# A decoder layer with a mixture of experts: the start and the end of the expert stage rearranged

## The chip, the cores and the metric

The kernel runs on one core of a Trainium2 chip. The metric is device time in microseconds (us), the median of several executions. The kernel's engines are named as in its profile: PE is the matmul engine (PEld its weight loads), DVE is VectorE, ACT is ScalarE, POOL is GpSimd, SP is SyncE, which here only issues transfers. All data is fp32.

## The reference

The input `x` has 2 x 1024 tokens of 256 numbers. Three blocks are added to it one after the other: self-attention of its normalised rows, cross-attention to 77 context rows, and a feed-forward block with experts. Only the last one is touched by the change:

```python
probs = jax.nn.softmax(flat @ gate_W, axis=-1)           # 8 experts
topk_w, topk_idx = jax.lax.top_k(probs, TOP_K)           # the best two
topk_w = topk_w / topk_w.sum(axis=-1, keepdims=True)
combine = (one_hot(topk_idx, n_exp) * topk_w[..., None]).sum(axis=1)
out = 0.5 * gelu(flat @ shared_W + shared_b)
for e in range(n_exp):
    h = gelu(flat @ W1[e] + b1[e])                       # 256 -> 1024
    out = out + combine[:, e:e+1] * (h @ W2[e] + b2[e])  # 1024 -> 256
out = (out - mean) * rsqrt(var + 1e-5) * gamma + beta
x = x + out
```

`flat` is the layer-normalised input of the block. Every token is needed by two experts only, with two weights.

## The kernel before

**Stages.** Self-attention runs from 0 to about 540 us, cross-attention with the layer norm, the gate and the routing to 665.8, the experts to 952.7, the end to 1002.9. In the first two stages the order of each engine's instructions is written out by hand (a list of words, worked off inside `manual_schedule`); this ends at L1351, and after it a scheduler orders the instructions by their dependences and by the order of the program.

**Routing.** Tokens stand in 16 groups (`NT`) of 128. The routing gives each (token, choice) pair, 4096 in all, a slot in a list that is sorted by expert and padded to multiples of 128. For each slot `rows()` (L1275) works out with four DVE instructions `to_row`, the pair's row in the DRAM buffer `pairs`, and from it `from_row`, the token's row in the DRAM buffer `xnd` of normalised tokens. An empty slot gets a `to_row` past the end, which the write leaves out. `owner_i` has the expert of each tile, and DVE wrote it earlier.

**Tiles.** The slots are worked off in 23 tiles: 12 pair tiles of 256 slots, then 11 single tiles of 128. How many of the last three are needed depends on the data (`count_i`), so tiles 20 to 22 lie inside branches. A tile consists of

- `fetch_weights` (L1336): SP loads the tile's expert number into a register and issues three transfers, `w1` (1 MB, L1339), `w2` (1 MB, L1342) and `b2` (128 KB, L1345). There are three sets of buffers. The sets of tiles 0 and 1 are asked for ahead of the routing's last steps, the set of tile i + 2 in tile i.
- `fetch` (L1391): POOL issues one indirect transfer for every 128 slots, which gathers rows of `xnd` by `from_row` (L1396). Three buffers `xg`, two tiles ahead.
- `first_layer` (L1406): PE transposes `xg` into `px` (L1412), DVE copies it to `xgT` (L1416), 16 matmuls give `ph` (L1422), ACT takes the Gelu with the bias (L1429).
- `second_layer` (L1434), one tile behind: 8 or 16 matmuls into `po` (L1441), DVE adds the bias into `y` (L1448), POOL issues an indirect transfer that scatters `y` to `pairs` by `to_row` (L1452).

Beside the tiles stand asides: the shared expert's Gelu in tiles 1 to 4, adding `beta` to the tokens `xs` in tiles 5 to 8, and in tile 9 `weigh` (L1362), which works out the two weights `wts` of each token.

**The end.** Eight transfers of 512 KB (L1508) load the pair rows: four chunks `c` of four groups of tokens, each for the first and for the second choice, on the queues of SP and ACT. Per chunk DVE adds the weighted rows to the shared expert's output `acc` with eight `scalar_tensor_tensor` (L1516) and takes mean and variance (L144, L145); `norm_scale` follows on DVE (L136) and POOL (L137). For chunks 0 to 2 DVE works out an offset (L1526), ACT normalises (L1530), and POOL multiplies by `gamma` (L1534) and adds the tokens (L1537). Chunk 3 does all this on DVE (`affine_residual`, L208 and L212). Each chunk's output leaves as one transfer of 512 KB (L1538).

Of the kernel before, what the change touches and what calls it, by code (L numbers as in the profile page):

```python
# [8 lines left out]
F32 = mybir.dt.float32  # L9
# [5 lines left out]
P = 128  # L15
# [25 lines left out]
def decoder_kernel(  # L41
# [48 lines left out]
    xnd = dram.tile([N, D], F32, name="xnd")  # L90
    pairs = dram.tile([2 * N, D], F32, name="pairs")
# [130 lines left out]
    scrap = const.tile([P, 6048], F32, name="scrap")  # L222
# [950 lines left out]
    pair_no = number("pair_no", [[N, 2], [P, NT]], 1, 1, [P, 2, NT])  # L1173
# [19 lines left out]
    pair = rt.tile([P, NS], F32, name="pair")  # L1193
# [81 lines left out]
    def rows():  # L1275

        ppk = held["ppk"]
        nc.vector.tensor_scalar(pair, ppk, 0.0, float(2 * N + 1), ALU.is_equal, ALU.mult)
        nc.vector.scalar_tensor_tensor(pair, pair, -1.0, ppk, ALU.add, ALU.add)
        nc.vector.tensor_copy(to_row, pair)  # L1280
        nc.vector.tensor_scalar(from_row, to_row, N - 1, None, ALU.bitwise_and)
# [46 lines left out]

    with tc.tile_pool(name="ff1", bufs=1) as ff1, ExitStack() as later:
        b2s = [ff1.tile([P, D], F32, name=f"b2_{k}") for k in range(3)]
        gamma_f = load_bcast(f_gamma, "gamma_f")
        beta_f = load_bcast(f_beta, "beta_f")
        def fetch_weights(i):  # L1336
            e = nc.sync.value_load(owner_i[0:1, i : i + 1], min_val=0, max_val=E - 1)
            w1, w2, b2 = w1s[i % 3], w2s[i % 3], b2s[i % 3]
            nc.sync.dma_start(  # L1339
                out=w1, in_=f_w1[bass.ds(e, 1)].rearrange("o (kc p) f -> p (o kc) f", p=P)  # L1340
            )
            nc.sync.dma_start(  # L1342
                out=w2, in_=f_w2[bass.ds(e, 1)].rearrange("o (hc p) f -> p (o hc) f", p=P)
            )
            nc.sync.dma_start(out=b2, in_=f_b2[bass.ds(e, 1)].to_broadcast([P, D]))  # L1345
            return w1, (w2, b2)

        weights = {i: fetch_weights(i) for i in range(2)}
# [29 lines left out]

        ff2 = later.enter_context(tc.tile_pool(name="ff2", bufs=1))
# [11 lines left out]
        def fetch(i):  # L1391

            w1, w2b2 = weights.pop(i) if i in weights else fetch_weights(i)
            xg = xgs[i % 3]
            for s, k in enumerate(blocks(i)):
                fetched[i] = nc.gpsimd.indirect_dma_start(  # L1396
                    out=xg[:, s, :],
                    out_offset=None,
                    in_=xnd[:, :],
                    in_offset=bass.IndirectOffsetOnAxis(  # L1400
                        ap=from_row[:, k : k + 1], axis=0
                    ),
                )
            return w1, w2b2, xg

        def first_layer(i, w1, xg):  # L1406
# [9 lines left out]
            nc.vector.tensor_copy(xgT, px)  # L1416
# [44 lines left out]
        def tiles(todo, last, got, behind):  # L1461

            for i in range(*todo):
                w1, w2, xg = got.pop(i)
                hT = first_layer(i, w1, xg)
                if behind is not None:
                    second_layer(*behind)
                if i + 2 < last:
# [10 lines left out]
        got = {0: fetch(0), 1: fetch(1)}  # L1479
        asides = {9: weigh}  # L1480
        for c in range(4):
            asides[1 + c] = lambda c=c: finish_shared(c)
            asides[5 + c] = lambda c=c: add_rows(c, beta_f)
        behind = tiles((0, 2), always + 2, got, None)
# [3 lines left out]
        def rest(upto):  # L1488
            second_layer(*tiles((always, upto), upto, dict(got), behind))

# [11 lines left out]
        land = [w.rearrange("p a f -> p (a f)") for w in w1s + w2s]  # L1502
        yts = {}
        for c in range(4):
            for i in range(2):
                yt = land[c][:, 4 * D * i : 4 * D * (i + 1)].rearrange("p (t d) -> p t d", d=D)
                r0 = N * i + 512 * c
                (nc.sync, nc.scalar)[i].dma_start(  # L1508
                    out=yt, in_=pairs[r0 : r0 + 512, :].rearrange("(t p) d -> p t d", p=P)
                )  # L1510
                yts[c, i] = yt
        for c in range(4):
            a4 = acc[:, 4 * c : 4 * c + 4, :]
            for t in range(4):
                for i in range(2):
                    nc.vector.scalar_tensor_tensor(  # L1516
                        a4[:, t, :], yts[c, i][:, t, :], wts[:, i, 4 * c + t : 4 * c + t + 1],
                        a4[:, t, :], ALU.mult, ALU.add,
                    )
            if c == 3:  # L1520
                affine_residual(a4, a4, c, gamma_f, 1e-5)
            else:
                mv = stats(a4, 4)
                r = norm_scale(mv, 4, 1e-5)
                off = small.tile([P, 4], F32, tag="off", name="off")
# [3 lines left out]
                for t in range(4):  # L1529
                    nc.scalar.activation(  # L1530
                        a4[:, t, :], a4[:, t, :], AF.Identity,
                        bias=off[:, t : t + 1], scale=r[:, t : t + 1],
                    )
                nc.gpsimd.tensor_tensor(  # L1534
                    a4, a4, gamma_f.unsqueeze(1).to_broadcast([P, 4, D]), ALU.mult
                )
                nc.gpsimd.tensor_tensor(a4, a4, xs[:, 4 * c : 4 * c + 4, :], ALU.add)  # L1537
            nc.sync.dma_start(  # L1538
                out=outf[512 * c : 512 * c + 512, :].rearrange("(t p) d -> p t d", p=P), in_=a4
            )  # L1540
# [37 lines left out]
```

## Time and profile before

| what | us |
|---|---|
| median of 3 runs (lowest to highest) | 1005.02 (1004.63 to 1005.73) |
| the profiled execution, its own time | 1004.62 |
| its span in the trace | 1002.9 |
| PE / DVE / ACT / POOL busy in the span | 894.6 / 594.9 / 536.1 / 403.9 |
| first gather issued | 669.63 |
| last transfer to the output issued | 997.98 |

The mean granted clock of PE is 0.956 of full speed in the profiled execution. Times on the timeline count from the start of the span. "A<-B" with a pair of names is an operation that writes A from B; in brackets stands how long the engine had been idle before it and what released it. The page of the profile gives long tables; the stretches and timelines that matter are shown where they are used.

### The profile page before, as it was taken

The page shows a single profiled execution, that of the slowest core. Times are in us where ns is not written, and L with a number is a line of the kernel's source. Part 1 is how long each engine was busy: PE and PEld are TensorE (multiplying, and loading weights), DVE is VectorE, ACT ScalarE, POOL GpSimd, SP SyncE. Part 2 cuts the span into 40 slices and gives each one's busy share as a digit, 9 for nine tenths or more (in the row PEclk, how much of TensorE's full clock was granted, in tenths as well). Part 3 has the DMA queues.
Part 4 walks back from the last instruction along what each step waited for, and adds up shares of the span by engine and source line. Part 5 has one row for each costly group of instructions (what it writes and reads, how often), then busy time and mean ns, then how long its engine had stood idle before and what let it go on. Part 6 is the DMA issues. An engine that isn't in the chain of part 4 may idle for free.

```text
span 1002.9 us, 15898 instructions
## 1 busy us (share of the span) xinstructions
PE 894.6 (89%) x5948; PEld 516.9 (52%) x5948; DVE 594.9 (59%) x1185; ACT 536.1 (53%) x1064; POOL 403.9 (40%) x336
## 2 busy tenths in 40 slices
PE   5999999999999999999946999979999999998900
PEld 2543433333333333333314667767788788887800
DVE  4876658877897787987589998760110110110057
ACT  3457667777887786887844777313322222233301
POOL 1533223553335544343466887023444421222125
PEclk9999999999999999999977999998999999998955
DMA  8200000000000000000000000146645645799152
GB/s 177 50 1 1 2 2 1 2 1 1 1 1 1 1 2 1 1 1 2 1 1 18 1 22 23 42 133 230 196 163 189 207 155 174 256 318 318 65 173 84
DMA packets 65143, 75.63 MB, mean 75 GB/s; under 512 B 17947, under 2 KB 57016, under 8 KB 65056
## 3 DMA queue, kind: packets, MB, share of 16 engines
q1 hardware_dynamic: 59040, 63.09, 19.9%
q0 software_dynamic: 3360, 8.79, 2.3%
q10 hardware_dynamic: 2656, 2.62, 0.8%
q8 instruction: 50, 0.82, 0.3%
q14 instruction: 37, 0.30, 0.1%
HBM read 66.10 MB, written 8.78 MB: 75 GB/s over the span
## 4 chain that ended last, share of the span: by engine, by line
PE 53%; DVE 14%; DMA 13%; issue 11%; POOL 6%; ACT 2%; POOLq 0%; ACTq 0%; DVEq 0%; SPq 0%
PE sA L525 15%; PE av L588 12%; DMA pairs<-y,to_row 11%; PE sB L571 11%; PE pp L495 3%; POOL pairs L1452 2%; PE pv L333 2%; DVE scrap L1516 2%; PE pb L387 1%; DVE cm L676 1%; PE ph L1422 1%; POOL xg L1396 1%; DVE cs L688 1%; PE pq L640 1%; DVE scrap L672 1%
## 5 line engine op out<-in xcount | busy, mean ns | idle before, releaser
L532 DVE TENSOR_REDUCE mx<-sA 128x1 f32<-128x512 f32 x512 | 317.5, 683 | 71.5 <-PE sB L571 63.8
L579 ACT ACTIVATE pt<-sB 128x512 f32<-128x512 f32 x512 | 264.6, 603 | 79.8 <-PE sB L571 79.6
L525 PE MATMUL sA<-kT,scrap 32*128 32x512 f32 x1024 | 259.2, 619 | 0.0
L601 POOL TENSOR_TENSOR avs<-avs,part 128x512 f32<-128x512 f32 x112 | 142.1, 1268 | 269.9 <-ACT part L600 264.6
L571 PE MATMUL sB<-qB,kT 32*128 32x512 f32 x1024 | 248.5, 616 | 0.0
L1429 ACT ACTIVATE hT<-ph,b1s 128x256 f32<-128x256 f32 (+1 forms) x184 | 77.8, 424 | 186.5 <-PE ph L1422 184.4
L525 PEld LDWEIGHTS sA<-kT,scrap 32*128 32x128 f32 x1024 | 101.5, 183 | 87.8 <-ACT pt L579 52.3
L1441 PE MATMUL po<-w,hT 128*128 128x256 f32 x560 | 139.2, 387 | 6.5 <-DVE y L1448 5.2
L1422 PE MATMUL ph<-xgT,w 128*128 128x256 f32 (+1 forms) x736 | 139.6, 336 | 2.0 <-ACT hT L1429 2.0
L588 PE MATMUL av<-pt,vaug 128*32 128x512 f32 x1024 | 137.4, 605 | 1.7 <-DVE mx L532 1.7
L1422 PEld LDWEIGHTS ph<-xgT,w 128*128 128x128 f32 x736 | 117.5, 193 | 26.7 <-ACT hT L1429 11.3
L1448 DVE TENSOR_TENSOR y<-po,b 128x512 f32<-128x512 f32 (+1 forms) x23 | 13.0, 564 | 187.1 <-PE po L1441 180.4
L571 PEld LDWEIGHTS sB<-qB,kT 32*128 32x128 f32 x1024 | 97.7, 183 | 38.4 <-issue 30.1
L1441 PEld LDWEIGHTS po<-w,hT 128*128 128x128 f32 x560 | 101.5, 192 | 21.3 <-DVE y L1448 8.3
L1452 POOL DMA_INDIRECT pairs<-y,to_row x35 | 35.5, 1016 | 123.9 <-DMA pairs<-y,to_row 82.5
L1396 POOL DMA_INDIRECT xg<-xnd,from_row x35 | 34.2, 976 | 100.0 <-PE px L1412 61.9
L588 PEld LDWEIGHTS av<-pt,vaug 128*32 128x32 f32 x1024 | 21.0, 109 | 98.8 <-DVE mx L532 85.3
L600 ACT COPY part<-av 128x512 f32<-128x512 f32 x108 | 65.6, 608 | 8.1 <-PE av L588 7.9
L137 POOL TENSOR_TENSOR rstd<-rstd,nhalf 128x4 f32<-128x4 f32 x20 | 21.7, 1086 | 68.3 <-DVE rstd L136 68.2
L193 PE MATMUL pxT<-ident,xn 128*128 128x128 f32 x96 | 18.2, 309 | 28.8 <-ACT xn L183 17.4
L495 PE MATMUL pp<-xnT,scrap 128*128 128x512 f32 x64 | 33.3, 648 | 0.4 <-DVE xnT L196 0.3
L705 ACT COPY PT<-ppT 77x512 f32<-77x512 f32 x64 | 32.4, 588 | 2.0 <-DVE xs L1052 1.0
(239 smaller groups left out, 958.3 us busy)
## 6 DMA issues: line engine op xcount, KB each, us to landing
w<-in_L_ffn_W_dram SPq DMA_DIRECT2D x46, 1024.0 KB, 7.4
b<-in_L_ffn_b_dram SPq DMA_DIRECT2D x23, 128.0 KB, 6.6
xs<-in_x_dram SPq DMA_DIRECT2D x4, 512.0 KB, 8.2
xnd<-xn SPq DMA_DIRECT2D x4, 512.0 KB, 2.9
w<-pairs SPq DMA_DIRECT2D x4, 512.0 KB, 9.4
w<-pairs ACTq DMA_DIRECT2D x4, 512.0 KB, 7.4
out_dram<-scrap SPq DMA_DIRECT2D x4, 512.0 KB, 2.9
mk<-in_mask_BxSxS_ik_dram SPq DMA_DIRECT2D x1, 616.0 KB, 6.0
```

Source lines behind the costliest of these rows:

```text
L495: nc.tensor.matmul(pp, lhsT=wqk[name][:, kc, P * G : P * G + P], rhs=xnT[:, kc, b * S + 512 * j : b * S + 512 * j + 512], start=(kc == 0), ...
L525: nc.tensor.matmul(s, lhsT=units[h // 4, "q"][r0 : r0 + 32, q0 : q0 + P], rhs=units[h // 4, "k", g % 2][r0 : r0 + 32, 512 * kh : 512 * kh ...
L532: nc.vector.tensor_reduce(largest[h][:, qt, hh : hh + 1, kh], s, AX.X, ALU.max)
L571: nc.tensor.matmul(s, lhsT=units[h // 4, "k", g % 2][r0 : r0 + 32, kt * P : (kt + 1) * P], rhs=shifted[h][r0 : r0 + 32, :], start=True, st ...
L579: nc.scalar.activation(powers[m, hh], s, AF.Exp, scale=1.0 / 16.0)
L588: nc.tensor.matmul(av[32 * hh : 32 * hh + 32, :], lhsT=vaug[:, kt, 4 * g + hh, :, b], rhs=powers.pop((m, hh)), start=True, stop=True,)
L600: copy(part, av)
L601: nc.gpsimd.tensor_tensor(sums[h], sums[h], part, ALU.add)
L1422: nc.tensor.matmul(ph[:, hc % group, :], lhsT=w1[:, kc, hc * P : (hc + 1) * P], rhs=xgT[:, kc, :], start=(kc == 0), stop=(kc == 1),)
L1429: hidden[i] = nc.scalar.activation(hT[:, hc, :], ph[:, hc % group, :], AF.Gelu, bias=b1s[:, i, hc : hc + 1])
L1441: nc.tensor.matmul(po[:, s, :], lhsT=hT[:, hc, s * P : (s + 1) * P], rhs=w2[:, hc, :], start=(hc == 0), stop=(hc == NH - 1),)
L1452: nc.gpsimd.indirect_dma_start(out=pairs[:, :], out_offset=bass.IndirectOffsetOnAxis(ap=to_row[:, k : k + 1], axis=0), in_=y[:, s, :], in_ ...
```

## The change

**Rows.** `rows()` has three DVE instructions. The numbers of the pairs begin at 2N, so that an empty slot's zero, after an exclusive-or with 2N, is past the end by itself; `from_row` is worked out second and `to_row` third.

**Weights.** There are four sets of buffers; the fourth lies in `xnT`, the transposed tokens, which nobody reads any more by then. Ahead of the routing's last steps SP asks only for `w1` of tile 0. After the two gathers of tile 0, SP issues a tiny transfer of two numbers of their result to a DRAM scrap `landed`, so SP waits for the gathers there; then come `w2` and `b2` of tile 0 and the sets of tiles 1 and 2. The set of tile i + 3 is asked for in tile i. POOL's gathers for tile 3 wait for `landed`, since it reads the buffer that they write.

**Diagonals.** In asides of tiles 10 to 13, 32 DVE `tensor_scalar` multiply the identity by a token weight each: for every group of 128 tokens and each choice a 128x128 matrix with the weights on its diagonal. In the order of the built program the 32 stand in a row on DVE, behind the weights `wts` and ahead of the next tile's `y`.

**End.** The order is written out. PE multiplies each 128x256 block of pair rows by its diagonal, both choices into one PSUM sum: 32 matmuls. For chunks 2 and 3 four identity matmuls put the shared expert's rows into the sum first, while the rows are on their way; for chunks 0 and 1 DVE adds these rows from PSUM. DVE takes the statistics, chunk 2 and 3 straight from PSUM. ACT normalises chunks 0 to 2, POOL multiplies chunks 0 and 1 by `gamma`, DVE chunk 2; DVE adds the tokens. Chunk 3 is again all DVE after the sum. Its output leaves in two halves.

```diff
-        nc.vector.tensor_scalar(pair, ppk, 0.0, float(2 * N + 1), ALU.is_equal, ALU.mult)
-        nc.vector.scalar_tensor_tensor(pair, pair, -1.0, ppk, ALU.add, ALU.add)
-        nc.vector.tensor_copy(to_row, pair)
-        nc.vector.tensor_scalar(from_row, to_row, N - 1, None, ALU.bitwise_and)
+        nc.vector.tensor_copy(pair, held["ppk"])
+        nc.vector.tensor_scalar(from_row, pair, N - 1, None, ALU.bitwise_and)
+        nc.vector.tensor_scalar(to_row, pair, 2 * N, None, ALU.bitwise_xor)
...
-        weights = {i: fetch_weights(i) for i in range(2)}
+        *first_set, second_of_0 = fetch_weights(0, 1)
+        weights = {0: tuple(first_set)}
...
+        def spread(c):
+            made[:] = [None]
+            for t in range(4 * c, 4 * c + 4):
+                for i in range(2):
+                    made[0] = nc.vector.tensor_scalar(
+                        weight(i, t), ident, wts[:, i, t : t + 1], None, ALU.mult
+                    )
...
-        got = {0: fetch(0), 1: fetch(1)}
+        got = {0: fetch(0)}
+        gate_in = nc.sync.dma_start(out=landed, in_=xgs[0][0:1, :, 0:1])
+        got[1] = fetch(1)
+        with tc.issue_after(gate_in.ins):
+            second_of_0()
+            weights[1] = fetch_weights(1)
+            weights[2] = fetch_weights(2)
...
+            def add_up(c):
+                for u in range(2):
+                    for t in range(2):
+                        for i in range(2):
+                            nc.tensor.matmul(
+                                summed[c, u][:, D * t : D * t + D],
+                                lhsT=weight(i, 4 * c + 2 * u + t), rhs=yts[c, i][:, 2 * u + t, :],
+                                start=(c < 2 and i == 0), stop=(i == 1 and (c < 2 or t == 1)),
+                            )
+            def add_shared(c):
+                for u in range(2):
+                    rows_u = rows_of(c, u)
+                    nc.vector.tensor_tensor(rows_u, rows_u, summed[c, u], ALU.add)
...
+            for c in (2, 3):
+                for u in range(2):
+                    nc.tensor.matmul(
+                        summed[c, u], lhsT=ident, rhs=rows_of(c, u), start=True, stop=False
+                    )
+            for c in range(4):
+                add_up(c)
+            add_shared(0)
+            measured(0)
+            add_shared(1)
+            shifted_by(0)
+            measured(1)
+            times_gamma_f(0, nc.gpsimd)
+            measured(2)
+            shifted_by(1)
+            plus_tokens(0)
+            times_gamma_f(1, nc.gpsimd)
+            measured(3)
+            shifted_by(2)
...
+            plus_tokens(1)
+            times_gamma_f(2, nc.vector)
+            plus_tokens(2)
```

Here `measured` takes the statistics and `rstd`, `shifted_by` works out the offset and has ACT normalise, `times_gamma_f` multiplies by `gamma` on the engine named, and `plus_tokens` adds the tokens and sends the chunk out. In the last gap stand chunk 3's four `scalar_tensor_tensor` with mean and `gamma`; behind the last line four with `rstd` and the tokens, with a transfer out behind every two.

## The prediction

> **What bounds the kernel now.** I read the busy time by engine for stretches cut at the stage borders first, then the timeline at the start of the experts, then at the end. The columns of the first view are: stretch, its length, busy time (and instructions) of PE, PEld, DVE, ACT and POOL, the granted PE clock, the share of the DMA engines, GB/s.
>
> ```profile
> core 0: us, PE busy (x) PEld busy (x) DVE busy (x) ACT busy (x) POOL busy (x), PEclk, DMA share, GB/s
> 665.80:680.40 14.60, 8.26 (x42) 6.49 (x43) 3.18 (x13) 1.50 (x3) 7.03 (x8) 0.87 0.93 320
> 680.40:853.00 172.60, 168.73 (x780) 139.63 (x778) 17.09 (x28) 50.52 (x101) 61.84 (x49) 0.99 0.54 183
> 962.80:998.00 35.20, 0.00 (x0) 0.00 (x0) 31.87 (x79) 6.22 (x12) 18.97 (x10) 0.50 0.37 119
> ```
>
> From 680.4 to 853 PE works 168.7 of 172.6 us: the pair tiles are bound by matmuls, whose number and order the change keeps. The two ends of the experts are different. Before 680.4 PE is half idle while the DMA engines are 93% busy; from 962.8 to 998.0 VectorE works 31.9 of 35.2 us and PE nothing. The change acts at these two places. The self-attention and cross-attention stages in front of 665.8 are untouched.
>
> The timeline at the start (start, length, engine, line, operation; in brackets the idle time before it and its releaser):
>
> ```profile
> 669.63 1.23 POOL L1396 DMA_INDIRECT xg<-xnd,from_row  x1 [31.00 <-PE psh L891]
> 673.68 0.95 POOL L1396 DMA_INDIRECT xg<-xnd,from_row  x1 [0.30 <-issue]
> 677.24 0.45 PE L1412 MATMUL px<-ident,xg 128*128 128x128 f32 x1 [3.97 <-DMA xg<-xnd,from_row]
> 679.74 0.90 PE L1412 MATMUL px<-ident,xg 128*128 128x128 f32 x3 [0.55 <-DMA xg<-xnd,from_row]
> 680.43 3.41 PE L1422 MATMUL ph<-xgT,w 128*128 128x256 f32 x8
> ```
>
> PE waits for the gathers of tiles 0 and 1 (two of 128 rows each). PE's order is transposes of tile 0, transposes of tile 1, first layer of tile 0, so it is the fourth gather, issued at 673.68 and landing at about 679.7, that releases the first real matmul at 680.43. A gather takes 7.5, 6.9, 6.1, 6.0 us from issue to landing here; the median of all is 6.9 and the shortest, on a quiet queue, 3.6. Six weight transfers (4.5 MB, asked from 665.8 on) share the engines with them.
>
> The timeline of the end:
>
> ```profile
> 956.34 3.27 SPq L1508 DMA_DIRECT2D w<-pairs  x4
> 962.77 3.26 DVE L1516 SCALAR_TENSOR_TENSOR scrap<-w,wts,scrap 128x256 f32<-128x256 f32 x8 [9.73 <-DMA w<-pairs]
> 972.15 2.34 POOL L1534 TENSOR_TENSOR scrap<-scrap,gamma_f 128x1024 f32<-128x1024 f32 x1 [2.38 <-ACT scrap L1530]
> 973.38 1.38 DVE L1516 SCALAR_TENSOR_TENSOR scrap<-w,wts,scrap 128x256 f32<-128x256 f32 x1
> 974.57 2.40 POOL L1537 TENSOR_TENSOR scrap<-scrap,xs 128x1024 f32<-128x1024 f32 x1
> 974.78 2.46 DVE L1516 SCALAR_TENSOR_TENSOR scrap<-w,wts,scrap 128x256 f32<-128x256 f32 x1
> 996.28 1.67 DVE L212 SCALAR_TENSOR_TENSOR scrap<-scrap,rstd,xs 128x256 f32<-128x256 f32 x4 [0.52 <-POOL rstd L137]
> ```
>
> The first chunk of pair rows lands at 962.75, and VectorE sets the pace from there: a weighted sum of 128x256 takes 0.37 us in a row (659 ns as the mean of all 32), but 1.38 and 2.46 us when a GpSimd pass over 128x1024 runs beside it. That is about 0.9 + 2.0 us in each of three chunks: 8.8 us of VectorE's time are spent blocked. The loads, issued together at 956.3, land by chunk at 962.7, 965.5, 968.5 and 971.8 (4.19 MB at the rate seen there) and are not the limit after the first.
>
> **The change, part by part: the start.** `rows()` has three VectorE operations in place of four, and `from_row` is the second, not the fourth: two operations of about 0.22 us less ahead of the first gather. So the gathers are issued at 669.18, 670.7, 672.0 and 673.2. With the weights of tile 0's second layer and of tile 1 held back until tile 0's gathers have landed, only 1 MB of weights runs beside them (asked at 665.8, landing in 4.9 us even now, so at 670.7). The gathers then have the engines nearly to themselves: I take the quiet 3.6 us, so the fourth lands at 676.8 rather than 679.7, and the first layer starts at about 677.4: -3.0 us. Bounds: -0.45 (landing still takes six us) to -3.0.
>
> On this gain stands the clock of PE. In the trace it falls to 0.50 at about 676.6 and comes back at 683.5. This makes the first eight `ph` records last 3.41 us, where such records take about 0.22 each warm.
>
> ```profile
> 918.00:920.00 2.00, 1.35 (x8) 1.04 (x8) 0.00 (x0) 0.45 (x2) 0.00 (x0) 1.00 1.00 391
> 920.00:922.00 2.00, 0.83 (x6) 0.60 (x6) 0.00 (x0) 0.73 (x2) 0.09 (x1) 1.00 1.09 385
> 922.00:924.00 2.00, 2.00 (x8) 1.32 (x8) 0.42 (x1) 0.00 (x0) 0.88 (x1) 0.61 0.91 256
> ```
>
> These rows (the stretch columns as above) show the clock falling at 922.6 after four microseconds in which PE was 42 to 68% busy and never idle for long. The Trainium skill ("TensorE: Matmul & The Clock Gate", "Part 1: The HAM clock gate") says that the gate closes after an idle window of about 3.4 us and opens after a busy one as long. After the change PE's longest idle stretch would be 673.3 to 674, so by the page the clock is never lost and the start is worth -3.8. By the rows a sparse stretch is enough, and between 673 and 677.4 PE does eight transposes. Cold from 677 until 680.0 it is -2.9, cold until 683.5 (windows that don't move with the work) -1.8. I take the row's side: **-2.4**, bounds -0.4 to -3.8.
>
> What may eat it: SyncE issues the tiny transfer to `landed` behind tile 0's weight address and six further register loads for tiles 1 and 2, and waits there for tile 0's second gather. It would land at about 674.4, the transfer takes a short hop, and the queue then issues `w2(0)`, `b2(0)`, set 1 and set 2. `w1(1)` is asked at 677 and, at the 4.9 us of `w1(0)`, lands at 682; it is needed after tile 0's first layer, at about 686.5. So there is 4.5 us of cover. `w2(0)` lands at 679 to 681 and is needed at about 694. GpSimd's gathers for tile 3 stand behind `landed` too, with tens of microseconds to spare.
>
> **Four sets of weights and the branch.** From tile 1 on PE works 14.95 us per pair tile and 7.3 to 8.1 us per single tile, and the chain of waits has no wait of PE on weights. Asking one tile earlier hides nothing that isn't hidden: **0**, with 1.5 us either way for the branch of the last tiles (917 to 932), where there are stalls[...] of about 1 us and half a clock, and where code and transfers are rearranged.
>
> **The diagonals.** 32 VectorE `tensor_scalar` of 128x128 follow the weights, in a row in VectorE's order. The weights are ready at 801.06 and the next `y`, on which PE's `po` buffer hangs, is at 808.21. The nearest row is a 128x128 `tensor_scalar` with two pointers, 0.256 us apart; with one, about 0.20. So 6.4 to 8.2 us in 7.15 us: late by 0 to 1.0, and up to 1 more if a GpSimd pass stands beside it. I take **+0.4**, bounds 0 to 2.
>
> **The end.** In place of 32 weighted sums on VectorE there are 4 matmuls of 512 columns ahead of the rows' arrival and 32 of 256. Two records of 0.22, 0.43 us warm, 0.86 cold. The first chunk's eight take 3.5 us warm, 6.9 cold. PE ends its identity matmuls at about 957 and idles until 962.75, longer than the 4.0 us after which the clock fell at 956.6 before; so it starts cold and warms in about 4 us: 4.65 cold and 3.35 warm, with two waits, some 6.0. The sum T of chunk 0 stands at 968.75. VectorE goes on from there, by its own rows: the add of the second half out of PSUM 0.73; four means and variances with their `rstd` 2.40 (6.04 to 8.44 in the first tokens' statistics); two adds 1.33; statistics of chunk 1 2.40 and of chunk 2 2.40: T+9.4. GpSimd takes `rstd` 1 before the gamma pass of chunk 0 (1.2 + 2.35), which therefore runs from T+8.2 to T+10.6. Then VectorE adds the tokens of chunk 0 (128x1024, twice the 0.69 of a 128x512, less the fixed part: 1.2) to T+11.8, statistics of chunk 3 to T+14.2, an offset and four 0.37 to T+15.8, chunk 1's tokens, chunk 2's gamma and tokens 3 x 1.2, and the last four 1.67: T+21.1, and T+21.9 with some 0.8 of gaps. GpSimd has one more gamma pass (T+12.7 to T+15.1). The skill ("GPSIMD Engine Reference", "1. Specifications") says that VectorE with two SBUF inputs or in a two-port mode contends with GpSimd, which speaks against the change: the offsets, `rstd` and 32 spreads are of this kind and were not seen alone. The row above, 1.38 beside GpSimd, agrees for two inputs. So by the page `off` 1 waits for chunk 0's gamma pass and `off` 2 for chunk 1's: T+22.9, and by ports left free T+21.9. I take T+22.9 = 991.65, where the old end is 997.95: -6.3; the last transfer out is 256 KB, not 512, -0.4. The part after it stays at 4.9 less that. **-6.7**; bounds -10 (warm all along, no port waits) to -1.6 (cold for two chunks, and a gamma pass that waits more).
>
> **Sum.** -2.4 + 0 + 0.4 - 6.7 = -8.7. The profiled execution took 1004.62 with a span of 1002.9: 995.9 with a span of 994.2. The median stands 0.4 above the profiled one, so 996.3.
>
> **The rivals.** *Better*: the clock is kept at the start or the ports do not block: -3.8 and -7.7 make some 992.5. For it: the page on the gate; against: the rows at 918 to 924. *Start worth nothing*: the gathers are bound by their own descriptors and take 6 us on a quiet queue too, and only 0.45 is gained: 998.3. The 3.6 us row is one gather, and the others also ran beside weights; that speaks against. *End half*: PE stays cold during chunks 0 and 1, each 128x256 matmul at 0.86, so that the sum of chunk 1 comes at 976.5 rather than 972, and the gain there is about 3: 1000.0. All 36 matmuls at half speed would make 27.5 us of them from 962.75, 990.3 for chunk 3, and the end as before: about 1003. *Slower*: weights held behind `landed` become the wait of PE. The gathers must land late for it: from `w1(1)` landing past 686.5 each us costs one. It begins when the hold is 4.5 us longer than worked out, and the whole gain is lost at 13 us; with tile 0's gathers at 689 it would be about 1006. The trace's landing times of at most 7.5 us speak against it.
>
> **How the numbers follow.** Forecast 0.58, better 0.15, start nothing 0.12, end half 0.07, as before or slower 0.08 (of this 0.03 within 0.2% and 0.05 slower). 0.2% (2 us) is what a measurement of this kernel can tell from no change. The sign: faster 0.92, same 0.03, slower 0.05. The forecast's own range is 993.3 to 999.5; with the better case's 992.5 (less 1.5 for the branch) and the half end, 990.5 to 1001.5.
>
> **What would show it.** Right: the first `ph` at 677 to 678 and a first-layer clock back at 680 to 683; gathers landing in about 3.6 us; PE's tile cadence at 14.95 us; VectorE's 32 spreads ending by 808; the diagonals of chunk 0 lasting 5 to 7 us from the landing; the last transfer issued 6 us sooner after the landing. Wrong: a wait of PE on `w` after tile 0; gathers of 6 us; matmuls of the end all at 0.86; adds of VectorE out of PSUM longer than 0.73, or GpSimd's passes blocking more than the offsets.

## The result, and the profile after

The changed kernel takes 989.26 us (median of 4 runs, 988.01 to 991.94) where the kernel before took 1005.38 beside it (1004.63 to 1007.47): a ratio of 0.9844, with a 95% interval of 0.9827 to 0.9860. That is 16.1 us less. The forecast was 8.7 less and a range down to 990.5, so the sign was right, and the time lies below the range. Two later measurements of the same kernel gave 993.2 and 990.87, both inside it; the median of all its 14 runs is 990.4, or about 14.4 us less than the kernel before.

The profiled execution took 991.94 with a span of 990.2, and is the slowest of the first four. The same view as before the change, busy time by engine for stretches, cut at the places that answer to the old cuts (columns: stretch, length, PE, PEld, DVE, ACT, POOL busy, granted PE clock, share of the DMA engines, GB/s):

```profile
core 0: us, PE busy (x) PEld busy (x) DVE busy (x) ACT busy (x) POOL busy (x), PEclk, DMA share, GB/s
665.70:678.90 13.20, 9.41 (x52) 7.35 (x52) 4.95 (x23) 1.76 (x3) 5.97 (x6) 0.99 0.42 136
678.90:852.00 173.10, 169.01 (x780) 139.49 (x778) 23.65 (x60) 50.53 (x101) 62.82 (x50) 0.99 0.61 212
960.00:985.80 25.80, 14.06 (x64) 12.06 (x64) 21.34 (x55) 6.09 (x12) 9.67 (x6) 0.87 0.45 155
```

The pair tiles are as before. In front of the first layer the DMA engines are now 42% busy, not 93%, and the stretch from the landing of chunk 0 to VectorE's last instruction is 25.8 us long, not 35.2, with 21.3 us of VectorE's work in it.

Lines of the timeline at the start of the experts:

```profile
671.31 1.23 POOL L1425 DMA_INDIRECT xg<-xnd,from_row  x1 [31.84 <-DVE mine L1284]
675.36 0.95 POOL L1425 DMA_INDIRECT xg<-xnd,from_row  x1 [0.30 <-issue]
676.08 1.08 PE L1441 MATMUL px<-ident,xg 128*128 128x128 f32 x5 [0.68 <-ACT scrap L899]
678.44 0.68 PE L1441 MATMUL px<-ident,xg 128*128 128x128 f32 x3 [1.27 <-DMA xg<-xnd,from_row]
678.92 3.48 PE L1455 MATMUL ph<-xgT,w 128*128 128x256 f32 x8
688.47 7.14 PE L1455 MATMUL ph<-xgT,w 128*128 128x256 f32 x32 [0.30 <-DMA w<-in_L_ffn_W_dram]
```

The fourth gather is issued at 675.36 and has landed by 678.44, 3.1 us later where it was 6.0. The eight cold `ph` records are still there (3.48 us), and tile 1's first layer now waits for its weights at 688.47, which it did not before. The wait is 0.30 us here; in two more traces of this kernel it is 0.41 and 0.95 us, as in this line of the third:

```profile
686.79 7.14 PE L1455 MATMUL ph<-xgT,w 128*128 128x256 f32 x32 [0.95 <-DMA w<-in_L_ffn_W_dram]
```

Lines of the timeline of the end:

```profile
953.28 3.70 PE L1628 MATMUL sum<-scrap,ident 128*128 128x512 f32 x8 [2.78 <-issue]
959.98 0.70 PE L1574 MATMUL sum<-w,scrap 128*128 128x256 f32 x2 [3.00 <-DMA w<-pairs]
963.74 1.29 DVE L1583 TENSOR_TENSOR scrap<-scrap,sum 128x512 f32<-128x512 f32 x2 [12.78 <-PE sum L1574]
972.10 2.34 POOL L1619 TENSOR_TENSOR scrap<-scrap,gamma_f 128x1024 f32<-128x1024 f32 x1
973.22 1.24 DVE L137 TENSOR_SCALAR rstd<-bnmv 128x4 f32<-128x4 f32 x1
984.16 1.67 DVE L1654 SCALAR_TENSOR_TENSOR scrap<-scrap,rstd,xs 128x256 f32<-128x256 f32 x4
```

The four identity matmuls (eight records) do not follow the last tile directly: PE stands idle for 2.78 us, and they run from 953.28 to 956.98. The timeline names no releaser, but the view of the line with the branch around the last tiles (`--source`: count, shortest, median and longest in ns, first and last start) does. The first of these two rows is from the kernel before, the second from the changed one:

```profile
L1496 PEldq COMPARE_BRANCH  x3: 69/362/3684, 921.3 to 951.9; - x3
L1544 PEldq COMPARE_BRANCH  x3: 69/362/3427, 919.6 to 949.8; - x3
```

PE's sequencer is in the last of these branches from 949.79 to 953.22. In all 14 traces it takes 3.4 to 3.85 us, and in all ten that have the identity matmuls these begin within 0.06 us of its end. What makes it so long is not shown. The idle time in front of the diagonals is then 3.0 us, and the diagonals run at full clock. VectorE is blocked beside GpSimd's gamma passes, but only in two small `rstd` instructions (1.24 and 1.20 us instead of 0.17), each of which ends within 0.02 us of the pass.

**Where the time went.** The routing's last matmul in front of the experts, `ppk` (it picks the slots' columns), is the last instruction that both kernels have in the same place. It starts at 667.24 and 666.69 in two traces of the kernel before, and at 669.37, 676.72 and 667.32 in three traces of the changed kernel, so what lies ahead of it scatters by itself. Behind it I cut at landmarks, and set apart the branch (from the `y` of tile 18 to that of tile 19), which also scatters. The first two landmarks, `ppk` and the first `y`, before and after:

```profile
667.24 0.41 PE L1273 MATMUL ppk<-pick,places 128*128 128x39 f32 x2 [1.74 <-DVE places L883]
703.54 0.69 DVE L1448 TENSOR_TENSOR y<-po,b 128x512 f32<-128x512 f32 x1 [4.76 <-PE po L1441]
669.37 0.41 PE L1274 MATMUL ppk<-pick,places 128*128 128x39 f32 x2 [1.74 <-DVE places L884]
702.56 0.69 DVE L1481 TENSOR_TENSOR y<-po,b 128x512 f32<-128x512 f32 x1 [4.76 <-PE po L1474]
```

| from, to (us) | before (2 traces) | changed (3 traces) | mean difference |
|---|---|---|---|
| `ppk` to first `y` | 36.3, 36.3 | 33.2, 33.5, 33.6 | -2.9 |
| first `y` to `y` of tile 18 | 213.7, 214.0 | 213.0, 213.0, 213.0 | -0.8 |
| branch | 14.3, 14.4 | 13.9, 11.9, 13.9 | set apart |
| tile 19 to last `y` | 21.1, 21.2 | 21.1, 21.2, 21.1 | 0 |
| last `y` to chunk 0's first use | 10.2, 8.9 | 9.5, 8.8, 9.2 | -0.4 |
| from there to VectorE's last end | 35.2, 35.2 | 25.8, 25.8, 25.8 | -9.3 |
| to the end of the span | 5.0, 5.0 | 4.3, 4.3, 4.3 | -0.6 |
| sum without the branch | 321.4, 320.4 | 306.9, 306.6, 307.0 | -14.0 |

So the traces show 14.0 of the 16.1 us of the first measurement. The other 2.1 must lie ahead of `ppk` and in the branch, which scatter by more than that; no trace shows them, since the executions in the middle of the two measurements were not profiled.

### The profile page after: what moved, and what is told of

It reads as the page before. It is cut to its first block, busy times and chain, and to the rows that moved or that the text cites. A ratio compares the mean times of both kernels' runs of the same rounds, so it can differ in the third digit from the quotient of the medians.

```text
span 990.2 us, 16048 instructions
## 1 busy us (share of the span) xinstructions
PE 915.1 (92%) x6020; PEld 532.6 (54%) x6020; DVE 590.8 (60%) x1192; ACT 536.4 (54%) x1064; POOL 394.5 (40%) x332
## 4 chain that ended last, share of the span: by engine, by line
PE 74%; DVE 15%; DMA 6%; ACT 2%; issue 1%; POOL 1%; SPq 0%; DVEq 0%; POOLq 0%; ACTq 0%
PE sA L526 15%; PE av L589 12%; PE po L1474 11%; PE ph L1455 11%; PE sB L572 11%; DMA pairs<-y,to_row 3%; PE pp L496 3%; PE pv L334 2%; PE pb L388 2%; DVE cm L677 1%; DVE cs L689 1%; PE pq L641 1%; DVE scrap L673 1%; DVE bnst L160 1%; DVE xs L1053 1%
## 5 line engine op out<-in xcount | busy, mean ns | idle before, releaser
L1455 PE MATMUL ph<-xgT,w 128*128 128x256 f32 (+1 forms) x576 | 109.3, 335 | 0.8 <-ACT hT L1462 0.3
L1474 PE MATMUL po<-w,hT 128*128 128x256 f32 x432 | 105.2, 382 | 3.4 <-DVE y L1481 3.3
L1455 PEld LDWEIGHTS ph<-xgT,w 128*128 128x128 f32 x576 | 92.0, 193 | 20.5 <-ACT hT L1462 7.7
L1474 PEld LDWEIGHTS po<-w,hT 128*128 128x128 f32 x432 | 77.7, 190 | 14.4 <-DVE y L1481 5.5
L1474 PE MATMUL po<-xnT,hT 128*128 128x256 f32 x128 | 33.2, 395 | 2.8 <-issue 1.5
```

Of the source, the lines that this page charges most:

```text
L1455: nc.tensor.matmul(ph[:, hc % group, :], lhsT=w1[:, kc, hc * P : (hc + 1) * P], rhs=xgT[:, kc, :], start=(kc == 0), stop=(kc == 1),)
L1474: nc.tensor.matmul(po[:, s, :], lhsT=hT[:, hc, s * P : (s + 1) * P], rhs=w2[:, hc, :], start=(hc == 0), stop=(hc == NH - 1),)
```

## The experiments

All are variants of the changed kernel unless said otherwise. "Rest" is the last row of the table above: from `ppk` to the end of the span without the branch. Ratios are to the kernel before on the same chip.

**The changed kernel again.**

> The changed kernel once more, unaltered. Theory: what the change moves lies behind the matmul that picks the slots' columns (ppk, the last common instruction of the routing). From its start to the end of the span the kernel before took 335.7 us (667.2 to 1002.9) and the changed one 320.8 (669.4 to 990.2): 14.8 less. The rest of the difference of the medians, 16.1, is in the time ahead of it, which differs from execution to execution. So this run should show 320.8 within 0.5 behind ppk, wherever ppk starts (667 to 670), and a time of 988 to 992. Rival: the part behind ppk differs by several us from execution to execution too, and the 14.8 is chance.

Median 993.2 (990.06 to 996.95), ratio 0.9858 (0.9796 to 0.9919). `ppk` started only at 676.72, and behind it came 318.5 us, not 320.8. The theory missed by 2.3 us: 1.9 of that is the branch, which took 11.9 us here and 13.9 before. So the part behind `ppk` does not repeat from execution to execution; the rest, 306.6 after 306.9, does.

**The end alone.** Old rows, three sets, no wait for gathers; diagonals and new end.

```diff
-            w1, w2, b2 = w1s[i % 4], w2s[i % 4], b2s[i % 4]
+            w1, w2, b2 = w1s[i % 3], w2s[i % 3], b2s[i % 3]
...
-        *first_set, second_of_0 = fetch_weights(0, 1)
-        weights = {0: tuple(first_set)}
+        weights = {i: fetch_weights(i) for i in range(2)}
...
-        gate_in = nc.sync.dma_start(out=landed, in_=xgs[0][0:1, :, 0:1])
```

> Only the diagonals and the new end; rows, three sets of weights and their asking as before. Theory (the end was worth more than forecast because PE's clock was not lost in front of the diagonals): 9.3 us less from the landing of chunk 0 to the last VectorE instruction, 0.6 less behind it, perhaps 0.7 sooner landing: 994.8 to 995.5, with chunk 0's eight matmuls in 3.5 us. Rival (the end is worth the forecast 6.7 and the rest of the gain is from the start and the four sets): 998.7.

Median 993.52, ratio 0.9892 (0.9816 to 0.9969). From the landing to VectorE's last end 25.8 us, and chunk 0's matmuls in 3.5: the end gives 9.3 us and not 6.7, by itself, and the rival is out; the median is 1.3 us below what the theory expected. The first `y` stands at `ppk` + 36.6, close to the 36.3 before.

**The start alone.** New rows, four sets, wait for the gathers; the end of the kernel before.

```diff
-            asides[10 + c] = lambda c=c: spread(c)
...
-            for c in range(4):
-                add_up(c)
+                    nc.vector.scalar_tensor_tensor(
+                        a4[:, t, :], yts[c, i][:, t, :], wts[:, i, 4 * c + t : 4 * c + t + 1],
+                        a4[:, t, :], ALU.mult, ALU.add,
+                    )
```

> Only the new rows, four sets and the weights held behind tile 0's gathers; no diagonals, the end as before. Theory (3.1 us less at the first y, 0.7 less in the single tiles and 0.4 in the branch): 1001.2, and 331.5 us behind ppk. Rival (start as forecast 2.4, four sets nothing): 1003.0.

Median 1000.13 of 16 runs, ratio 0.9960 (0.9938 to 0.9983). First `y` at `ppk` + 33.1 (before: 36.3), end 35.2 as before. Behind `ppk` stand 329.0 us, 2.5 less than expected, and they contain a short branch of 11.7; the rest, 317.4, is 3.0 to 4.1 less than before. The two halves add up: 11.3 less (end alone, 309.6 against the mean 320.9) and 3.5 less make 14.8, where both together gave 14.0.

**Without the wait for tile 0's gathers.**

```diff
-        *first_set, second_of_0 = fetch_weights(0, 1)
-        weights = {0: tuple(first_set)}
+        weights = {i: fetch_weights(i) for i in range(2)}
...
-        got = {0: fetch(0)}
-        gate_in = nc.sync.dma_start(out=landed, in_=xgs[0][0:1, :, 0:1])
-        got[1] = fetch(1)
...
+        got = {0: fetch(0), 1: fetch(1)}
+        weights[2] = fetch_weights(2)
```

> The changed kernel without the wait for tile 0's gathers: the sets of tiles 0 and 1 are asked for as in the kernel before, set 2 behind the gathers of tiles 0 and 1; four sets and the new end stay. Theory (holding the weights is what lets the gathers land in 3.2 us): the fourth gather takes 6 us again and lands about 2.8 us later relative to ppk, so 991.5 to 992.5. Rival (the shorter gathers are from the earlier issue alone): no change, 989.3.

Median 991.49, ratio 0.9878 (0.9805 to 0.9950), which by time alone can't be told from the changed kernel. The timeline tells it:

```profile
671.42 1.24 POOL L1424 DMA_INDIRECT xg<-xnd,from_row  x1 [31.86 <-DVE mine L1284]
672.97 0.95 POOL L1424 DMA_INDIRECT xg<-xnd,from_row  x1 [0.31 <-issue]
679.41 0.45 PE L1440 MATMUL px<-ident,xg 128*128 128x128 f32 x1 [3.89 <-DMA xg<-xnd,from_row]
682.10 3.72 PE L1454 MATMUL ph<-xgT,w 128*128 128x256 f32 x8
```

The gathers leave as early as in the changed kernel, but PE gets the first only 8.0 us after its issue, and the first layer starts at `ppk` + 12.6, not + 9.5. So it is the held weights that let the gathers land in about 3 us, as the prediction had it, and the earlier issue is worth only its 0.45. The first `y` comes at + 35.8, 2.4 later than with the wait.

**Without the identity matmuls.** The rows of the shared expert are missing from chunks 2 and 3.

```diff
-            for c in (2, 3):
-                for u in range(2):
-                    nc.tensor.matmul(
-                        summed[c, u], lhsT=ident, rhs=rows_of(c, u), start=True, stop=False
-                    )
...
-                                start=(c < 2 and i == 0), stop=(i == 1 and (c < 2 or t == 1)),
+                                start=(i == 0), stop=(i == 1),
```

> The changed kernel without its four identity matmuls: the shared expert's rows of chunks 2 and 3 are left out of the sums (so this part of the output is missing its share), nothing takes their place. Theory (they break PE's idle time in front of the diagonals into two pieces of about 3 us, too short for the clock to fall): PE idles 9 us, its clock falls to 0.50, the eight matmuls of chunk 0 take 5.5 to 6.9 us, not 3.5, and the last VectorE instruction ends 28 to 29.2 us after chunk 0's landing, not 25.85. Rival (the clock is kept anyway, or the extra time is hidden): 25.85.

The timeline and two stretches of this kernel (stretch columns as above; the clock stands third from the end):

```profile
957.67 1.22 PE L1574 MATMUL sum<-w,scrap 128*128 128x256 f32 x2 [8.49 <-DMA w<-pairs]
958.68 1.06 PE L1574 MATMUL sum<-w,diag 128*128 128x256 f32 x2
964.30 1.28 DVE L1583 TENSOR_TENSOR scrap<-scrap,sum 128x512 f32<-128x512 f32 x2 [14.66 <-PE sum L1574]
```

```profile
953.00:954.00 1.00, 0.00 (x0) 0.00 (x0) 0.00 (x0) 0.00 (x0) 0.00 (x0) 0.64 0.01 4
...
963.00:964.00 1.00, 1.00 (x5) 0.86 (x4) 0.00 (x0) 0.00 (x0) 0.00 (x0) 0.74 1.09 384
```

PE idles 8.5 us, its clock falls at 953.3 and comes back at 963.5, and the first add comes 6.6 us after the landing, not 3.8; VectorE ends 28.7 us after it. The median of two runs is 992.0, ratio 0.9866 (0.9846 to 0.9887). These 28.7 us come close to what the prediction had written for the changed kernel (28.9, with the sum at 6.0 and 22.9 behind it), though the parts are 6.6 and 22.1, so two misses cancel in it. The forecast of the end thus fits an end whose clock is lost; four matmuls that were put there to add the shared rows take that loss away, and save 2.9 us. This is one trace, but 8.5 us of idle time hold a whole idle window of the 3.41 us that the last section finds, wherever its grid lies.

**The kernel before, once more.**

> The kernel before once more, for a second trace of it. Theory: the part behind ppk without the branch (from the y of tile 18 to that of tile 19) is a property of the program: 321.4 us (335.7 less 14.3) within 0.5, except for 0.7 us in tile 14, where the first trace has a y that came 0.7 us later than in every kernel since, and which is chance; so 320.7 to 321.4. The branch takes either about 11.8 or about 14.2 us, by whether PE's clock falls in it. Rival (four sets of weights bring those 0.7 us): tile 14 takes 8.0 us here again, not 7.3.

One run, 1003.11; rest 320.4, branch 14.4. Tile 14 took 8.3 us here and 8.0 in the first trace, so this is not chance in one trace; the theory as I had put it falls.

**Three sets of weights.** Set i + 2 asked for in tile i, all else as changed.

```diff
-            w1, w2, b2 = w1s[i % 4], w2s[i % 4], b2s[i % 4]
+            w1, w2, b2 = w1s[i % 3], w2s[i % 3], b2s[i % 3]
```

> The changed kernel with three sets of weights in place of four, set i + 2 asked for in tile i as in the kernel before; the wait for tile 0's gathers, the rows and the new end stay. Theory (the fourth set hides nothing that was not hidden: the tiles of the kernel with only the new end, which has three sets, take as long as those of the changed one): relative to ppk the first y at 33.2 to 33.5, that of tile 18 213.0 later; from ppk to the end without the branch 306.5 to 307.0. Rival (with the weights asked for about 10 us later than before, three sets leave PE waiting in tiles 1 to 4): the first y's come more than 14.95 us apart and the part behind ppk is 1 to 3 us longer.

Median 991.99, ratio 0.9866 (0.9849 to 0.9882). First `y` at + 33.0, the pair tiles 14.95 us apart, rest 306.7: the rival is out, no tile waits for weights. But tile 16 took 8.1 us, not 7.3:

```profile
898.83 0.42 DVE L1479 TENSOR_TENSOR y<-po,b 128x256 f32<-128x256 f32 x1 [6.79 <-DMA pairs<-y,to_row]
```

This `y` waits for an earlier scatter to leave its buffer. One single tile like this, 0.7 to 1.0 us late, is in three of the four traces with three sets (both of the kernel before, and this one) and in none of the ten with four. That the fourth set calms the DMA queues at that place fits, but the kernel with the end alone has three sets and no such tile, so it is not shown.

**Tile 1's first weights ahead of tile 0's second ones.**

```diff
-            second_of_0()
-            weights[1] = fetch_weights(1)
+            *first_of_1, second_of_1 = fetch_weights(1, 1)
+            weights[1] = tuple(first_of_1)
+            second_of_0()
+            second_of_1()
```

> The changed kernel with one transfer moved: behind the wait for tile 0's gathers, the first weights of tile 1 are asked for ahead of the second weights of tile 0. Theory (what tile 0 gains is partly given back because PE waits for these weights): no wait of PE on weights, and the first y 0.3 to 0.9 us sooner relative to ppk: 32.5 to 32.9, where two executions of the changed kernel showed 33.2 and 33.5. Rival (the loss is clock and table load alone): 33.2 to 33.5 again, or later, if tile 0's second weights now come late.

Median 987.5, ratio 0.9829 (0.9797 to 0.9862). PE no longer waits for weights, and the first `y` stands at + 32.5, as the theory had it, 0.7 to 1.1 us sooner than in the three traces of the changed kernel. So about 1 us of the start's gain had been given back; 0.3 to 0.95 of it shows as the wait itself. The clock is still lost.

**And PE kept busy at the start.**

```diff
+            if i == 0:
+                idle = big("idle")
+                for k in range(3):
+                    nc.tensor.matmul(
+                        idle[:, k % 2, :], lhsT=ident, rhs=xg.rearrange("p s d -> p (s d)"),
+                        start=True, stop=True,
+                    )
```

> The kernel w1_first with three more matmuls of 512 columns on PE, of no use to the result, behind the transposes of tile 0; the built order then also has half of tile 0's first layer ahead of tile 1's transposes. Theory (PE's clock falls at the start for too little work in one window of 3.4 us): the clock stays at 1.00 from 676 to 684, the first eight records of ph take 1.8 us, not 3.4, and the first y comes at ppk + 31.0 to 31.8. Rival (the next limit is a transfer, the weights of tile 1 at ppk + 17 or the table load on ScalarE): no more than 0.3 us sooner than w1_first.

The clock stays at 1.00 from 675 to 684 and the first eight `ph` records take 1.89 us, not 3.5. But the first `y` comes at + 32.0, 0.5 sooner than in the kernel above, not 0.7 to 1.5: PE then waits 0.59 us for ScalarE, whose table load (1.28 us, at 677.46) begins only when the first `ph` is there. Median 989.85, ratio 0.9849 (0.9832 to 0.9867); the branch took 15.7 us in this trace.

**The early table, and a finer end.** To the kernel above come a small activation ahead of ScalarE's last copy of the routing, a PSUM tile for each half chunk, and another order on VectorE.

```diff
-                halves_of = big("sum") if c < 3 else None
-                for u in range(2):
-                    summed[c, u] = halves_of[:, u, :] if c < 3 else two("sum")
+                for u in range(2):
+                    summed[c, u] = sums.tile([P, 512], F32, tag="sum", name="sum")
...
+        nc.scalar.activation(early, b1s[:, 0, 0:1], AF.Gelu)
...
+            half_measured(2, 1)
+            scaled(2)
+            shifted_by(1)
+            half_measured(3, 0)
+            shifted_by(2)
+            plus_tokens(0)
+            times_gamma_f(1, nc.gpsimd)
+            half_measured(3, 1)
```

> The kernel warm_w1 with two more changes: ScalarE's table for the Gelu is loaded by one small activation ahead of its last copy of the routing, and in the end every half of a chunk has a PSUM tile of its own, so that VectorE adds and measures a half as soon as its four matmuls are done, chunk 3's first half is measured early, and the offsets and variances stand where GpSimd is not in its gamma pass. Theory (VectorE waited for all eight matmuls of a chunk because the sum was one tile, and was blocked 2 x 1.1 us beside GpSimd): from chunk 0's landing to the last VectorE instruction 23.0 to 24.6 us, not 25.85; first y at ppk + 31.0 to 31.6; without the branch 302.5 to 304.5 us from ppk to the end, where the changed kernel has 306.7. Rival (the passes of GpSimd block VectorE as before, only elsewhere): 25.3 to 25.9.

The end took 24.4 us, rest 304.1, both within the theory; the first `y` at + 32.5 did not. The table is loaded early, but the built order of this kernel has all of tile 0's first layer ahead of tile 1's transposes, and PE waits for ScalarE between its parts (0.27 and 0.35 us). Median 990.26, ratio 0.9861 (0.9817 to 0.9904): no gain that the time shows.

**The changed kernel a third time, and the better pieces together**, on one chip: tile 1's weights first, and the finer end of the last kernel, without the idle matmuls and the early table (the diffs are those shown).

> The changed kernel a third time, for five rounds beside w1_end on the same chip. Theory: 988 to 992, and 306.5 to 307.0 us from ppk to the end without the branch; chunk 0's eight matmuls in 3.5 us again, since what keeps PE's clock (four identity matmuls that begin about 2.8 us behind the last tile) is in the program. Rival: the clock in front of the diagonals was kept by luck in the executions seen so far, and once in a while it is not: 6.6 us from the landing to the first add, not 3.8.

> The kernel w1_first with the end of the kernel best (a PSUM tile for every half chunk, VectorE's order changed), without the idle matmuls and without the early table load. Theory (the two gains add up: 0.7 to 1.0 at the first y, 1.4 in the end): first y at ppk + 32.5, 24.4 us from the landing to the last VectorE instruction, 304.5 to 305.2 us from ppk to the end without the branch, and a time 2 us below that of third. Rival (the scatter of the time ahead of ppk and of the branch hides it): a difference of the medians within 1 us, whatever the trace shows.

The changed kernel: 990.87 (989.95 to 997.02 in 6 runs), ratio 0.9864 (0.9828 to 0.9901), rest 307.0, first add 3.8 us after the landing for the third time. The other: **984.55** (984.29 to 989.04), ratio 0.9799 (0.9765 to 0.9832), rest 303.6. It beats both kernels. VectorE's view of its end:

```profile
956.67 0.69 DVE L1639 TENSOR_TENSOR scrap<-scrap,sum 128x512 f32<-128x512 f32 x1 [10.42 <-PE sum L1577]
958.48 0.66 DVE L1639 TENSOR_TENSOR scrap<-scrap,sum 128x512 f32<-128x512 f32 x1
966.66 1.17 DVE L137 TENSOR_SCALAR rstd<-bnmv 128x4 f32<-128x4 f32 x1
976.45 1.67 DVE L1690 SCALAR_TENSOR_TENSOR scrap<-scrap,rstd,xs 128x256 f32<-128x256 f32 x4
```

The first add stands 2.1 us after the landing (954.58), since it waits for four matmuls and not eight; one of the two blocked `rstd` is left, the other was moved to a place without a gamma pass. The end takes 23.5 us. Both theories' numbers were a little too high here: 0.9 us for the end, 0.9 for the rest. The medians differ by 6.3 us where 2 were expected; the rest of the two traces shows 3.5 of them and their branches 1.4, and the remainder is scatter that no trace shows.

## Why the prediction was wrong

**The start** (-2.4, measured -2.9). The parts are of the kind forecast: the rows give 0.45 at the first gather, gathers land in 3.1 us because the weights are held back, and the clock is still lost, as the row's side of the weighing had it. Their sizes were off in ways that cancel. The first layer begins 3.6 to 3.8 us sooner, not 3.0. The clock stays low from 678.71 to 682.13, or `ppk` + 9.3 to + 12.8, which is the earlier of the two returns that were weighed. And the cover of 4.5 us for tile 1's weights was not there. SyncE issued them in time (`ppk` + 9.4, worked out 9.8), but they took 9.6 us to land and not the 4.9 of tile 0's first weights, which I had taken for them: tile 0's second weights stood ahead of them on the same queue. The mechanism of the "slower" rival was thus at work, at a price of about 1 us. A clock kept at the start is worth 0.5 us in the kernel with the idle matmuls, where the working had 0.9.

**The experts** (0, measured -0.8). One single tile with a late scatter in the kernel before is gone; what removed it stays open.

**The diagonals** (+0.4, measured 0). They ran 0.195 us apart, from 800.00 to 806.5, beside no GpSimd pass, and the next `y` came 14.95 us after the last one. The stated estimate of 0.20 was right, and the lateness that I took on top was not there.

**The end** (-6.7, measured -9.9, and -0.4 for the landing). This is the step that failed. The text said: "PE ends its identity matmuls at about 957 and idles until 962.75, longer than the 4.0 us after which the clock fell at 956.6 before; so it starts cold and warms in about 4 us". What it had wrong is when PE works in front of the diagonals, and so the clock that they find. Counted from the last tile's last matmul, the prediction has the identity matmuls end 4.4 us later, close behind it; they end 6.5 us later, since PE's sequencer first needs 3.4 us for its way out of the branch. That branch takes 3.7 us in the profile of the kernel before as well, and was in no term. The gap in front of the diagonals is then 3.0 us in this trace and not 5.75, the clock is full, and the first add stands 3.8 us behind the landing, not 6.0. The kernel without these matmuls has it at 6.6 and ends 2.9 us later. Even where the clock falls beside them, they bring it back in time (last section). That the branch moves them toward the landing was nobody's plan; no run has them right behind the last tile, so what the delay is worth is not shown.

Of the 3.2 us that the end was off, 2.2 are thus the first add. VectorE's chain behind it is 0.8 shorter than forecast, 22.1 us where 22.9 was written, and the span's tail 0.2. The two places where VectorE is blocked are there (about 1.05 us each), only that `rstd` stands ahead of the offsets and took the blocking. The chain also holds the add of chunk 0's first half, which the working had ahead of T: VectorE waits for all eight matmuls of a chunk.

**The range.** All five terms missed on the same side. With -14.0 in place of -8.7 the sum is 991.0, outside the forecast's own range (993.3 to 999.5). A clock that is not lost in front of the diagonals stood only in the bounds of the end (-10, measured -9.9) and in no rival: "better" was a clock kept at the start or ports that do not block, and neither came. Some of its sums are also off: -3.8 and -7.7 make 993.5 and not 992.5, 992.5 less 1.5 is 991.0 and not 990.5, and the matmuls that take 27.5 us from 962.75 are 32, not 36. The last step from 991.0 to the measured 989.26 is scatter of a few us ahead of `ppk` and in the branch, which was in no term at all; by that chance the first measurement fell below the range, and the two later ones did not.

## What to carry to other kernels

Before costing a matmul that follows a wait, ask what PE did in the few microseconds in front of it, and when that work really starts. Look at the sequencer's branches for that, not only at the engine's own instructions. Work that is put into an idle time for another reason can hold the clock there or bring it back, and taking it away shows how much that is worth. A transfer that is held back to let another one through is late itself: order what is released by when it is needed. Where one wait covers a tile, a smaller tile is a shorter wait.

## What the runs showed of the hardware

**PE's clock falls on a grid of 3.41 us.** In each of the 14 traces all falls of the clock in the stretches from 530 to 580, 620 to 710 and 910 to 960 us lie a whole number of 3.413 us apart. In the changed kernel they are at 542.18, 624.10, 641.17, 654.82, 678.71 and 924.47: between the last two lie 72 steps. The Trainium skill ("TensorE: Matmul & The Clock Gate", "Part 1: The HAM clock gate") states a free-running window of 3413 ns, which agrees. It also says that the clock is lost after an idle window; here it is lost after windows that are far from idle, too. These are windows of the changed kernel that end with a fall (the first two) and without (the others):

```profile
675.31:678.72 3.41, 1.36 (x9) 0.84 (x9) 0.69 (x1) 0.59 (x1) 2.75 (x3) 1.00 0.46 124
921.07:924.48 3.41, 1.73 (x10) 1.40 (x10) 0.12 (x1) 0.37 (x1) 1.13 (x2) 1.00 0.16 44
951.76:955.17 3.41, 1.89 (x5) 0.94 (x6) 0.00 (x0) 0.00 (x0) 0.45 (x1) 1.00 0.17 37
955.17:958.59 3.42, 1.81 (x5) 0.50 (x3) 0.00 (x0) 0.00 (x0) 0.00 (x0) 1.00 0.91 285
```

PE was busy 40% and 51% in windows that lost the clock, and 55% and 53% in windows that kept it. In the experts and the end of all 14 traces the clock fell after every window with less than 44% and after none with more than 57%; between the two it did either. In the stage ahead of them (620 to 663 us) windows of 63 to 91% lost it too, among them one of 84 or 85% in each of the 14 traces. In the changed kernel that is the one up to 654.82, in which PE works on matmuls of 8 to 128 columns and no transposes. Busy time is not all that counts there.

**This makes executions differ.** In the branch the clock fell in nine traces, and they took 13.9 to 15.7 us for it; in the five where it didn't fall, 11.7 to 12.4. Ahead of `ppk`, the seven traces without a fall between 620 and 650 have `ppk` at 666.6 to 667.3; two with one fall, at 622.3 and 623.7, have it at 667.3 and 668.8; four with falls at about 624.4 and 641.5, at 669.4 to 669.9; one with falls at 624.9, 648.8 and 662.5, at 676.7. The program there is the same but for a few small instructions. In front of the diagonals the clock was kept in three of the ten traces that have the identity matmuls, two of them of the changed kernel. In the other seven it fell 0.3 to 1.4 us behind the end of PE's branch, for one window, and was back 0.9 to 3.0 us before the first diagonal. So it was in the execution with `ppk` at 676.7, where it fell at 959.4:

```profile
959.00:961.00 2.00, 1.83 (x3) 0.84 (x4) 0.00 (x0) 0.00 (x0) 0.00 (x0) 0.61 0.07 19
961.00:963.00 2.00, 2.00 (x3) 0.79 (x3) 0.00 (x0) 0.00 (x0) 0.00 (x0) 0.53 0.84 191
963.00:965.00 2.00, 1.56 (x4) 0.38 (x2) 0.00 (x0) 0.00 (x0) 0.00 (x0) 1.00 1.08 372
```

So they hold the clock or reopen it, as the grid falls, and the first add came 3.8 us after the landing in every trace of the changed kernel. The reason given with the run without them, pieces of idle time too short for the clock to fall, does not hold: it fell beside such pieces in seven traces, and PE's work in between brought it back.
